# FiLM products by ranges of features, two transposes for the folding products, and a new order of work in a two-layer linear-attention kernel

## The chip, the cores and the metric

The kernel runs on one NeuronCore of one Trainium2 chip. The metric is device time in microseconds of one execution, lower is better. A change is judged against the median of the executions of the kernel before.

## What is computed

Two layers of the same form run one after the other on `x` of shape (32, 128, 512): 32 sequences of 128 positions with 512 features. Layer 0 has 16 heads of 32 features, layer 1 has 8 heads of 64. The masks differ a little; the rest is the same. Cut to what matters:

```python
xn = layernorm(x) * ln_w + ln_b
q, k, v = xn @ Wq + bq, xn @ Wk + bk, xn @ Wv + bv      # k and v masked by position
q = softmax(q per head, over the head's features)
k = softmax(k, over the positions)
att = einsum('bnhd,bnhl->bhdl', k, v)                    # head by head
y = einsum('bnhd,bhdl->bnhl', q, att).reshape(b, t, d)
emb_out = silu(emb) @ W_emb + b_emb                      # FiLM: emb is (32, 1024), W_emb is (1024, 1024)
scale, shift = split(emb_out, 2)
h = layernorm(y) * ln2_w + ln2_b
h = silu(h * (1 + scale) + shift) @ W_out + b_out
x = x + h
```

`emb_out` is the FiLM part. It is computed once for each layer, for all 32 sequences at once: a contraction over 1024 inputs (8 chunks of 128) for 1024 features and 32 rows.

## The kernel before

**Jobs.** The work is cut into 32 jobs: 16 pairs of sequences (`G = 2`) in layer 0, then the same 16 pairs in layer 1. The output of layer 0 goes through DRAM buffers `x1`. All data is float32. Function `job` records one job: normalise the input tile `z`, turn it over into `xnT`, make `k` (tiles `bank_ka`, `bank_kb`, `bank_kc`, `bank_ke`), softmax it, make `q` and `v` (`bank_qa` and so on), multiply `k` by `v` head by head (`bank_pa`), put the results on the diagonal of `att`, multiply by `q` (`bank_py`), normalise `y`, turn it over, apply FiLM and silu into `hT`, make the output (`bank_oa` and so on) and add it to the residual tile `x`.

**Seven products for eight.** In 31 of the 32 jobs each of the three large multiplications is done as seven products of half matrices instead of eight. `sums` forms the sums of halves of the activations (`Sx`, `Sh`, on GpSimd) and `sum_w` those of the weights (VectorE). Products 1, 6 and 7 go into the same PSUM bank `A` one on top of the other, 5 and 3 into bank `E`. Between two products of one bank another engine must have copied or added the bank's content: `kcopy` on ScalarE (line 671), `kadd`, `qcopy`, `qadd` and `oadd` on VectorE. The first job (`plain`) makes the eight products directly (`bank_kp`, `bank_qp`).

**Turning over.** Jobs 1 to 30 (`far`) turn tiles over with VectorE's 32x32 transposes and a round trip through DRAM (`moved`: one write, four reads on the SyncE queue). The first and the last job use TensorE transposes (`bank_xtp`, `bank_tq`, `bank_tk`, `bank_htp`); so does the input of job 1.

**FiLM.** `film` runs once for each layer. For each half `h` of the features and each half of the contraction it loads a 1 MB weight tile `we` and issues four products of 512 columns into `bank_em`, one in each of TensorE's four column groups (lines 479 to 490). Column group `j` holds contraction chunk `j` of the half, so each bank holds four partial sums for 512 features, in 32 partitions each. ScalarE copies the two banks (512 columns each) to the tile `y_e`. Then eight products with a folding matrix `fold` (four 32x32 identities, one above the other; made at the start by `make_fold`, line 373) add up the four partial sums and turn the result over at once, into `bank_etp` (line 498). Five VectorE instructions make the factors `fa` and `fc` of the layer from it.

**Order.** Nothing is issued as it is recorded. `Plan.op` takes each operation with its engine, an assumed duration (`mm`, `dve`, `act`, `pool`) and a due time: the job's base, `31 us` for each job, plus a number at the call, plus a shift from the table `SHIFT`. A row of the table belongs to one call of `op`, its entries to the instances in a job, and its columns to stages of the run: five of them (set-up, job 0, the rest of layer 0, layer 1, the last job). `schedule` then plays the engines in assumed time and picks on each engine, among the operations that can start first, the one due earliest. An operation on another engine's result can start a margin later than the result's assumed end; the margin `SAFE` depends on the engine that makes it (PE 1.35, VectorE 0.01, ScalarE 0.59, GpSimd 0.14, SyncE's transfers 5.62 us). The result is one fixed order of instructions in each engine's queue, and each queue runs strictly in that order.

Of the kernel before, what the change touches and what calls it, by code (L numbers as in the profile page):

```python
# [9 lines left out]
F32 = mybir.dt.float32  # L10
# [6 lines left out]
P = 128  # L17
# [21 lines left out]
    0: ([5.7, 15.9, 47.2, 55.2, 54.4, 44, 62.4, 10.5, 44.1, 62.3], [], [-97.3, -25.3, -45.3, 5.4, 3.3], [53.1, 30.1], []),  # L39
    1: ([], [0.2], [], [], []),  # L40
    2: ([], [27.5], [], [], []),
    3: ([], [-71], [], [], []),
    4: ([], [-16.5], [], [], []),
    5: ([-25.2, 10.4, 32.2, -41.2, 37.7, 6.8, 5.8, 67.3, 87.9, 16.6, -57.5, 31.4], [], [], [-45.1, -59.7, 21.8, -35.8, 14.5, -29, 63.3, 90.6, 5.3, -1.1, -112.2, 10.5], []),
    6: ([], [59.5, 36.8, 59, -24.3, -23.8, -28, 30.3, -17.4, 15.3, -49.7, 36, 7.5], [], [51, 7.4, -32, 18, -64.7, 11.6, 34.3, 28.1, 12.6, 49.7, 53, -39.4], []),
    7: ([-19.6, -17.7], [-47], [-9.4, 28.6], [-38.6, -54.5], [-19.8, -24.4]),
    8: ([-11.2], [], [], [], []),
    9: ([45.5], [], [], [], []),
    10: ([-0.6], [], [], [], []),
    11: ([-22.4], [], [], [], []),  # L50
    12: ([-51.4], [], [], [], []),
    13: ([-16.2, -62.4, 26.5, -36.5], [], [-40.9, -12.9, -23.3, -40.4], [], []),
    14: ([-108.7, -90], [], [2.1, -83.4], [], []),
    15: ([-8.7], [], [4.6], [], []),
    16: ([104.7], [], [41.1], [], []),
    17: ([-29.4], [], [12.6], [], []),
    18: ([-33.1], [], [-51.6], [], []),
    19: ([20.1], [], [57.8], [], []),
    20: ([-16.7], [], [36.6], [], []),
    21: ([98.9], [], [], [], []),  # L60
    22: ([], [-244.7, -141.5, -194.2, -240], [-97.7, -109.1, -130.8, -137, -128.4, -206.2, -333.8, -173.1], [-234, -348.8, -167.7, -71.2, -96.9, -232.6, -243.8, -66.1], [-155.9, -151.5, -127.9, -39.1, -50.7, -147.4, -192, 41.1]),
    23: ([], [], [-39.5, -46.3, -86.4, -246.7], [39, 14.5, 54.9, -63.1], []),
    24: ([], [], [-442.5, -175.6, -223.2, -214.2, -19.7, -47, -249.3, -177.4, -120.6, -199.8, -136, 23.1, -68, -42.8, -24.2, -36.8], [-275.7, -16, -45, 5.7, 48.7, -52.7, -15.7, 46.8, -28.9, -88.2, -92.5, 37.2, 72.2, 63.1, 131.9, 135.8], []),
    25: ([], [96.7, 54.3, 89.8, 65.9], [88.1, 56.4, 71.5, -129.6], [64.2, -41.9, 37.3, -69.5], [152.4, 66.9, 140, 66.9]),
    26: ([], [66.8, 227.4, 94.7, 169.7], [3.6, 121.5, -20.7, 168.3], [92.2, 115.2, 108.5, 168.7], [80.2, 202.2, 126.3, 200.5]),
    27: ([], [-6.3, 19, 65.2, 46.1], [-64.1, -98.9], [-75.4, -19.4], [94.2, 6.6, 70.6, 26.7]),
    28: ([], [-11.3, 64.1, 55.6, 58.2], [-62.3, -13.5], [-12, 223.4], [17.8, 102.7, 102.6, 77.2]),
    29: ([], [], [-38.4, -89.4, -183.3, -77.8], [23.2, -63.7, -92.9, 63], []),
    30: ([], [-91.4, -115.5, -85.1, -68.9], [], [], [-38.6, 6.3, -36.5, -24.9]),
    31: ([], [], [-19.6, 86.2, -70.8, -37.7], [-54.5, 128.2, -100.3, 28.5], []),  # L70
    32: ([], [32], [10.7], [], []),
    33: ([], [], [], [-12.2], [-23.9]),
    34: ([], [-56.2, -118.9], [-3.2, -130.3], [45.7, -29.6], [101.9, 27.4]),
    35: ([], [], [-31.3, -75.6], [133.6, 25.2], []),
    36: ([], [], [-13.5, 0.1, -36.6, 4], [-128.7, -99.9, -92.6, -75.9], []),
    37: ([], [-38, -89.5], [-24.8, -163], [], [10.1, -34.1]),
    38: ([], [16.5, 4, 1.9, -110], [11.8, -31, -3.3, -139.7], [], [-38.3, 29.3, 15.9, -81.1]),
    39: ([], [], [-98.8, -44.3, -29.9, -52.2, -126.4, -36.4, -55.1], [-94, -63.4, -46.1, -24.4, -46, -74.5, -116.1], [-18.2, -14.4, 6.4, 25.4, -11, -12.8, -89.6]),
    40: ([], [], [-135.6, 157.4, 1.7, -182.5, -172.5, 27.1, -156.9, -41.7], [-76.8, -104.5, -102.7, -356.7, -171, -108.9, -44.5, -149.9], [-118.2, -29.9, -61.7, -151.9, -160.7, -51.6, -81.6, -45.2]),
    41: ([], [], [-126.4, -120.8, -91.1, -70.4], [-16.2, -213.7, -208.6, -161.7], [102.4, 6, -7.7, 98.9]),  # L80
    42: ([], [-41.7, -48.3, -58.3, -3.8], [], [], []),
    43: ([], [-36.2, -44.2, 40.1, 28.7], [], [], []),
    44: ([], [19.5, 13.6], [-29.7, 2.1], [-65.6, 73.5], [45.4, 152.5]),
    45: ([], [92.5, -64.9], [-36.9, 13.7], [120.4, 62.2], [56, 143.4]),
    46: ([], [278.9, 169.5, 298.1, 241.9, 215.5, 187.7, 142.9, 298.2], [115, 86.1, 224.4, 228.8, 87, 168, 13.2, 217.3], [132.2, 170.4, 25, 189.7, 235.5, -17.3, 201.8, 243.1], [143.2, 156.6, 168.9, 220.9, 115.8, 118.2, 205, 231.9]),
    47: ([], [-51.7, -40.4], [-41.9, 50], [-168.9, -50.7], [24.8, 27.8]),
    48: ([], [1.5, -27.8], [-51.1, 43.9], [], []),
    49: ([], [], [-33.9, -20.6, -58.3, -10.5, -51.5, -14, -90.1], [-12.2, -35.7, -129.9, -10.7, -150.4, 14.7, -112.4], [107.2, 50.5, 90.7, 151.4, -5.8, 121.5, 87]),
    50: ([], [], [-115.7, -262, -215.8, -197.2], [-66.2, -119.4, -113, -255.5], [58.9, -39.6, 37.1, -113.1]),
    51: ([], [], [-79.6, -42.4, -38.3, -194.8], [-267.2, -385.2, -56.5, -311.8], [-113.2, -76.9, 39.7, -82]),  # L90
    52: ([], [-6.5, 5.2, 9.7, 0.7], [], [], []),
    53: ([], [-28.8, 70.1, -73.2, -24.9], [], [], []),
    54: ([], [53.8, 14.6], [107.1, 142.1], [62.6, -55.6], [140.3, 39.5]),
    55: ([], [-12.9, -44.2], [-30.4, -7.4], [-134.5, -105.7], [-5.9, -86.7]),
    56: ([], [24.2, 12.7], [148, 18], [110.2, 14.9], [150.8, 29.7]),
    57: ([], [-100, -59.5], [-40.2, -215.5], [-57.4, -206.5], [-147.7, 1.5]),
    58: ([], [40.6, -61.7], [58.7, -16.6], [37.6, 22.2], [22.5, 7.6]),
    59: ([], [], [183.4, 30.9], [31.8, 14.3], []),
    60: ([], [], [-63.4, -83.3], [-101.2, -40.5], []),
    61: ([], [54, 121.7], [], [], [88.4, 149.7]),  # L100
    62: ([], [-56.9, -89.1], [], [], [17.4, -47.9]),
    63: ([], [], [24.3, 101.9], [-74.4, -69.5], []),
    64: ([], [85.7, 89.8], [], [], [139.6, 132.8]),
    65: ([], [-95.5, 6.2], [], [], [-37.4, -11]),
    66: ([], [], [], [115.8, -5.1], [16.1, 16.5]),
    67: ([], [24.2], [-66.9], [-103.1], [64.6]),
    68: ([], [91.6, 110.8, 183.2, 28.2], [-19, 34.9, 122.6, 85.8], [], []),
    69: ([], [], [], [-216.7, -240], [-56, -56.5]),
    70: ([], [36.1, 28.6], [-35.5, 19.3], [1.9, -13.1], [61.1, 83.2]),
    71: ([], [-97.2, -39.7], [-173.2, -59.1], [79.7, -119.9], [81.5, 35.6]),  # L110
    72: ([], [], [58.4, 74.4], [118.1, -5], []),
    73: ([], [-75.6, -118.7], [], [], [-36.9, 28.2]),
    74: ([], [-54.5, -51, -83.3, -145, -53.1, -97.2, -81.4, -72.6], [], [], [20.4, 27.6, 36.9, 20.3, 36.4, 12.3, 19.1, -17.8]),
    75: ([], [], [-215.3, -73.1, -108.6, -101.3, -218.9, -167.7, 16.8, 73.8], [-79, -52.3, -191.4, -5.4, -172.2, -78.4, -21.9, 11.5], []),
    76: ([], [18, 16.6, -37.2, -72.2, 56, -24.7, -24.1], [-153.1, -119.4, -159.2, -107.5, -78.7, -115.4, -58.7], [34.2, -35.5, 48.4, 58.4, 57.7, 56.7, -41.8], [126.5, 33.1, 102.9, 80.4, 130.3, 111.6, 94.8]),
    77: ([], [], [], [43, -26.8, -32.4, -4], [18.5, 41, 19.2, 99.5]),
    78: ([], [19.2, 65.2, 30.1, -77.5, -50.7, -22.4, -160, -35.8], [-16.1, 29.3, -4.5, -119.2, -5, -41.5, -138, 18.5], [183.1, 215.1, 162.9, -57.4], [178.7, 285.7, 140.9, 0.5]),
    79: ([], [-62.8], [-25], [15.9], [28.4]),
}


class Buf:


    def __init__(self, kind, name):
        self.kind, self.name = kind, name
        self.ap = None
        self.left = 0
        self.free_at = 0.0
# [23 lines left out]
class Plan:  # L153

    HOP = {"PE": 0.17, "DVE": 0.07, "ACT": 0.07, "POOL": 0.07, "SP": 0.07}

    SAFE = {"PE": 1.35, "DVE": 0.01, "ACT": 0.59, "POOL": 0.14, "SP": 5.62}  # L160
    TAIL = {"PE": 0.13, "DVE": 0.08, "ACT": 0.12, "POOL": 0.08, "SP": 0.0}

    STEP = 31.0

    def __init__(self, nc):
        self.nc = nc
# [136 lines left out]
def dve(n):  # L303
    return 0.074 + n / 970
# [710 lines left out]
```

## Time and profile before

| what | value |
|---|---|
| three executions | 918.66, 919.46, 919.67 us; median 919.46 us |
| the profiled execution | 919.49 us, of which 917.7 us from the first to the last instruction |
| TensorE (PE) | busy 898.7 us, 98% of the span, 6294 matmul records |
| VectorE (DVE) | 767.5 us, 84% |
| ScalarE (ACT) | 633.6 us, 69% |
| GpSimd (POOL) | 535.1 us, 58% |
| DMA | 199.07 MB, mean 217 GB/s |
| FiLM products, `bank_em` | 64 records of 128x512, 32 a layer, in four groups of eight |
| folding products, `bank_etp` | 32 records of 128x32, 16 a layer |

One float32 product is two records in the trace, a TensorE transpose is one. A record's duration is the time from its start to its result; records of one stream overlap, so what a stretch of products costs is read from the start of its first record to the start of what follows. A row of the timeline is: start, duration (us), engine, line, operation, output<-inputs, shapes, number of records, and in brackets the idle time of the engine before it and what ended it.

### The profile page before, as it was taken

Reading aid. Unit: us, or ns where it says so; the run is one execution under the profiler, and the core shown is the slowest. Engines: PE = TensorE matmul, PEld = TensorE weight load, DVE = VectorE, ACT = ScalarE, POOL = GpSimd, SP = SyncE. Lnnn points to the kernel's source line nnn. Section 1 sums busy time; section 2 is a strip of 40 time slices with the busy share of each in tenths; the row PEclk is TensorE's granted clock in tenths of the full one; section 3 lists DMA queues with packets and bytes.
Section 4 is the critical chain, followed back from the end, with each engine's and each line's share of the span. In section 5 each row is a group of like instructions: output and inputs, shape, how many; then the busy total and the mean of one; then the engine's idle time right before and its main releaser. Section 6 shows DMA issues by size and latency. Waiting matters only on the chain.

```text
span 917.7 us, 18442 instructions
## 1 busy us (share of the span) xinstructions
PE 898.7 (98%) x6294; PEld 638.7 (70%) x6294; DVE 767.5 (84%) x1623; ACT 633.6 (69%) x1567; POOL 535.1 (58%) x741
## 2 busy tenths in 40 slices
PE   5999999999999999999999999999999999999996
PEld 4557776767777767776866677677767768676765
DVE  3888879878888888888998989889989879968775
ACT  4467768678687678786677577859778674586581
POOL 3665666656665666665656455457556544554554
PEclk9999999999999999999999999999999999999999
DMA  9747678897977576789776776868688592917542
GB/s 322 241 140 246 179 226 249 240 257 230 276 229 230 179 219 203 236 238 279 234 230 206 256 217 194 253 223 252 215 250 249 170 273 83 266 67 232 176 131 83
DMA packets 126701, 199.07 MB, mean 217 GB/s; under 512 B 13328, under 2 KB 78352, under 8 KB 126608
## 3 DMA queue, kind: packets, MB, share of 16 engines
q1 hardware_dynamic: 126608, 197.90, 69.8%
q8 instruction: 50, 0.82, 0.4%
q14 instruction: 43, 0.35, 0.1%
HBM read 118.68 MB, written 79.17 MB: 216 GB/s over the span
## 4 chain that ended last, share of the span: by engine, by line
PE 98%; DVE 1%; DMA 1%; issue 0%; POOL 0%; SPq 0%; ACT 0%; ACTq 0%
PE bank_qa L739 17%; PE bank_qe L739 12%; PE bank_ka L665 9%; PE bank_oa L913 9%; PE bank_py L868 6%; PE bank_ke L665 6%; PE bank_oe L913 6%; PE bank_qb L739 6%; PE bank_qc L739 6%; PE bank_kc L665 3%; PE bank_oc L913 3%; PE bank_kb L665 3%; PE bank_ob L913 3%; PE bank_pa L847 3%; PE bank_qp L754 1%; PE bank_kp L685 1%
## 5 line engine op out<-in xcount | busy, mean ns | idle before, releaser
L710 POOL TENSOR_TENSOR kT<-kT,mb 128x512 f32<-128x512 f32 x64 | 81.9, 1280 | 93.5 <-DVE kT L676 83.7
L717 ACT ACTIVATE kT<-kT,kmax 128x128 f32<-128x128 f32 x256 | 99.7, 391 | 47.8 <-DVE kmax L713 47.0
L671 ACT ACTIVATE kT<-bank_ka,cols_c 128x128 f32<-128x128 f32 x248 | 76.8, 362 | 74.1 <-PE bank_ka L665 67.5
L739 PE MATMUL bank_qe<-wqv,Sx 128*128 128x512 f32 x248 | 117.2, 595 | 0.0
L739 PE MATMUL bank_qa<-wqv,Sx 128*128 128x512 f32 x248 | 117.0, 594 | 0.0
L780 POOL TENSOR_TENSOR q<-q,qmax 128x512 f32<-128x512 f32 x64 | 66.9, 1046 | 67.6 <-DVE qmax L779 63.4
L899 ACT ACTIVATE hT<-yb,fc_c,fa_c 128x128 f32<-128x128 f32 x240 | 98.8, 482 | 0.4
L553 POOL TENSOR_TENSOR Sx<-xnT 128x256 f32<-128x256 f32 x62 | 44.3, 730 | 57.5 <-PE bank_qe L739 38.7
L553 POOL TENSOR_TENSOR Sh<-hT 128x256 f32<-128x256 f32 x64 | 47.4, 745 | 49.7 <-ACT hT L899 46.9
L739 PEld LDWEIGHTS bank_qa<-wqv,Sx 128*128 128x128 f32 x248 | 45.1, 190 | 42.3 <-issue 38.5
L739 PEld LDWEIGHTS bank_qe<-wqv,Sx 128*128 128x128 f32 x248 | 45.2, 190 | 41.9 <-issue 37.5
L665 PEld LDWEIGHTS bank_ke<-Sx,wk 128*128 128x128 f32 x496 | 63.0, 192 | 14.5 <-issue 11.7
L665 PEld LDWEIGHTS bank_ka<-Sx,wk 128*128 128x128 f32 x496 | 63.3, 192 | 10.5 <-issue 8.4
L868 PEld LDWEIGHTS bank_py<-att_c,qT 128*128 128x128 f32 x512 | 63.6, 192 | 9.6 <-issue 6.7
L633 ACT ACTIVATE xnT<-zb,cols_c 128x256 f32<-128x256 f32 x116 | 61.4, 593 | 10.2 <-PE bank_qc L739 8.8
L868 PE MATMUL bank_py<-att_c,qT 128*128 128x128 f32 x512 | 66.6, 276 | 1.5 <-DVE att_c L856 1.5
L913 PE MATMUL bank_oe<-wo,Sh 128*128 128x256 f32 x256 | 65.9, 380 | 1.7 <-DVE x L923 1.7
L913 PE MATMUL bank_oa<-wo,Sh 128*128 128x256 f32 x256 | 66.0, 381 | 0.8 <-DVE x L919 0.7
L665 PE MATMUL bank_ka<-Sx,wk 128*128 128x128 f32 x496 | 65.9, 276 | 0.0
L665 PE MATMUL bank_ke<-Sx,wk 128*128 128x128 f32 x496 | 65.8, 276 | 0.0
L595 ACT ACTIVATE y<-y,nmrb,rstdb 128x512 f32<-128x512 f32 x60 | 46.7, 805 | 25.9 <-POOL nmrb L583 25.8
L782 ACT ACTIVATE q<-q 128x512 f32<-128x512 f32 x64 | 40.1, 627 | 28.7 <-POOL q L780 28.4
(131 smaller groups left out, 2272.7 us busy)
## 6 DMA issues: line engine op xcount, KB each, us to landing
x<-x SPq DMA_DIRECT2D x32, 512.0 KB, 4.3
qd<-qb SPq DMA_DIRECT2D x30, 512.0 KB, 4.0
kd<-k SPq DMA_DIRECT2D x30, 512.0 KB, 4.2
qb<-qd SPq DMA_DIRECT2D x120, 128.0 KB, 3.4
k<-kd SPq DMA_DIRECT2D x120, 128.0 KB, 3.4
yd<-yb SPq DMA_DIRECT2D x30, 512.0 KB, 3.7
yb<-yd SPq DMA_DIRECT2D x120, 128.0 KB, 3.8
zd<-zb SPq DMA_DIRECT2D x29, 512.0 KB, 3.9
```

Of the source, the lines that this page charges most:

```text
L553: op(22, "POOL", pool(2 * T), lambda i=i, x=x, y=y, f=f: nc.gpsimd.tensor_tensor(S.ap[:, i], x(), y(), f), r, [(S, i)], due=due, lock=True)
L595: op(31, "ACT", act(512, 2, False), lambda: nc.scalar.activation(dst.ap[:, b, :], src.ap[:, b, :], AF.Identity, bias=nmr.ap[:, b : b + 1], ...
L633: op(36, "ACT", act(GT, 2, False), lambda c=c: nc.scalar.activation(xnT.ap[:, c, :].rearrange("p (b r t) -> p r b t", b=G, r=4), zb.ap[:, ...
L665: nc.tensor.matmul(t.ap[:, m * T : (m + 1) * T], kw[quarter].ap[:, c, m * P : (m + 1) * P], a()[:, c, :], start=(first and m == 0 and c == ...
L671: op(40, "ACT", act(T, 1), lambda m=m: nc.scalar.activation(kT.ap[:, 2 * h + m, i, :], Ak.ap[:, m * T : (m + 1) * T], AF.Identity, bias=co ...
L710: op(44, "POOL", pool(2 * GT), lambda hs_=hs_: nc.gpsimd.tensor_tensor(kT.ap[:, hs_].rearrange("p m b t -> p m (b t)"), kT.ap[:, hs_].rear ...
L717: op(46, "ACT", act(T, 1, False) + 0.093, lambda m=m, b=b: nc.scalar.activation(kT.ap[:, m, b, :], kT.ap[:, m, b, :], AF.Exp, bias=km.ap[: ...
L739: nc.tensor.matmul(t.ap, a()[:, c, :], wqv[quarter].ap[:, c, :], start=(first and c == 0), stop=(c == 1), skip_group_check=not first)
L780: op(55, "POOL", pool(512, False), lambda qh=qh, qm=qm: nc.gpsimd.tensor_tensor(qh(), qh(), qm.ap[:, :H].unsqueeze(2).to_broadcast([P, H, ...
L868: nc.tensor.matmul(py.ap[:, m * P : (m + 1) * P], qTc(b, m), att.ap[:, b, m, :], start=True, stop=True)
L899: op(75, "ACT", act(T, 2, False), lambda c=c, b=b: nc.scalar.activation(hT.ap[:, c, b * T : (b + 1) * T].rearrange("p (r t) -> p r t", r=4 ...
L913: nc.tensor.matmul(t.ap[:, :hf], a()[:, c, :], ow[quarter].ap[:, c, :], start=(first and c == 0), stop=(c == 1), skip_group_check=not first)
```

## The change

Three parts. First, in `film` each column group now takes a range of 128 features and the whole contraction: 16 products of 128 columns where there were four of 512. A bank then holds finished sums, 128 columns wide. Second, the copies to `y_e` are 128 columns wide, and two TensorE transposes take the place of the eight products with `fold`; `fold` and `make_fold` are gone. Third, the order is made anew: the `SHIFT` table has new values and eight stages instead of five, and the margins `SAFE` are changed. The calls of `op` after the removed one are numbered one lower.

```diff
 SHIFT = {
-    0: ([5.7, 15.9, 47.2, ...], [], [-97.3, ...], [53.1, 30.1], []),
...
+    0: ([9.3, 8.8, 89.5, ...], [], [], [-101.5], [-101.5, ...], [87.6, 38.9], [87.6], []),
...
-    SAFE = {"PE": 1.35, "DVE": 0.01, "ACT": 0.59, "POOL": 0.14, "SP": 5.62}
+    SAFE = {"PE": 1.21, "DVE": 0.00, "ACT": 0.37, "POOL": 0.31, "SP": 4.87}
...
-        stage = 0 if job < 0 else 1 if job == 0 else 2 if job < B // G else 3 if job < 2 * B // G - 1 else 4
+        stage = 0 if job < 0 else 1 + (job > 0) + (job > 1) + (job > 3) + (job >= B // G) + (job >= 2 * B // G - 2) + (job == 2 * B // G - 1)
...
-    fold = fixed("fold", [P, B])
...
-    def make_fold():
-        for j in range(P // B):
-            nc.vector.tensor_copy(fold.ap[j * B : (j + 1) * B, :], ident.ap[j * B : (j + 1) * B, j * B : (j + 1) * B])
-    op(3, "DVE", 0.5, make_fold, [ident], [fold])
...
                 def go(h=h, half=half, w=w):
                     for j in range(4):
-                        nc.tensor.matmul(
-                            e[h].ap[j * B : (j + 1) * B, :],
-                            cT.ap[:, 4 * half + j, :],
-                            w.ap[:, j, :],
-                            start=(half == 0),
-                            stop=(half == 1),
-                            tile_position=(0, j * B),
-                        )
+                        for g in range(4):
+                            nc.tensor.matmul(
+                                e[h].ap[g * B : (g + 1) * B, :P],
+                                cT.ap[:, 4 * half + j, :],
+                                w.ap[:, j, g * P : (g + 1) * P],
+                                start=(half == 0 and j == 0),
+                                stop=(half == 1 and j == 3),
+                                tile_position=(0, g * B),
+                            )
...
-            op(14, "ACT", act(512), lambda h=h: nc.scalar.copy(esb.ap[:, h, :], e[h].ap), [e[h]], [(esb, h)], due=14)
+            op(13, "ACT", act(P), lambda h=h: nc.scalar.copy(esb.ap[:, h, :P], e[h].ap[:, :P]), [e[h]], [(esb, h)], due=14)
...
         def total():
-            for c in range(NE):
-                nc.tensor.matmul(
-                    tp.ap[:, c * B : (c + 1) * B], esb.ap[:, c // NC, c % NC * P : (c % NC + 1) * P], fold.ap, start=True, stop=True
-                )
-        op(15, "PE", mm(NE, B), total, [esb, fold], [tp], due=15)
+            for h in range(2):
+                nc.tensor.transpose(tp.ap[:, h * P : (h + 1) * P], esb.ap[:, h, :P], ident.ap)
+        op(14, "PE", mm(2, P, True), total, [esb, ident], [tp], due=15)
```

## The prediction

> **What bounds the kernel now.** I read the page first, for the engine whose time the end hangs on:
>
> ```profile
> PE 898.7 (98%) x6294; PEld 638.7 (70%) x6294; DVE 767.5 (84%) x1623; ACT 633.6 (69%) x1567; POOL 535.1 (58%) x741
> ...
> PE 98%; DVE 1%; DMA 1%; issue 0%; POOL 0%; SPq 0%; ACT 0%; ACTq 0%
> ```
>
> The chain that ended last is TensorE for 98% of the span. The busy time by stages (columns: stretch, its length, PE, PEld, DVE, ACT, POOL, granted clock, DMA share, GB/s) and TensorE's waits tell where the rest is:
>
> ```profile
> 0.00:14.34 14.34, 4.04 (x16) 3.10 (x16) 6.29 (x16) 4.67 (x8) 5.12 (x17) 1.00 0.86 288
> 14.34:36.00 21.66, 21.66 (x98) 15.46 (x98) 12.47 (x22) 11.69 (x32) 11.93 (x14) 1.00 0.94 328
> 36.00:885.00 849.00, 848.97 (x6006) 601.30 (x6005) 731.53 (x1548) 604.30 (x1494) 504.09 (x694) 1.00 0.71 218
> 885.00:917.70 32.70, 24.01 (x178) 18.82 (x176) 17.20 (x39) 12.99 (x37) 13.95 (x18) 0.98 0.27 91
> ```
>
> ```profile
> PE bank_xtp L644 <- DVE z L591: 9.1, 1, 9.1
> PE bank_oe L913 <- DVE x L923: 1.7, 2, 1.1
> PE bank_py L868 <- DVE att_c L856: 1.5, 1, 1.5
> PE bank_xtp L644 <- ACT z L595: 1.1, 1, 1.1
> PE bank_oa L913 <- DVE x L919: 0.7, 1, 0.7
> ```
>
> From 14.3 to 885 us TensorE is never idle; all its waits are in the first 13 and the last 30 us. So a microsecond taken out of TensorE's stream anywhere ends the kernel a microsecond earlier, a new order can win only at the two ends, and in the middle it can only lose.
>
> **The change, part by part.** The sum is made against the profiled execution, 919.49 us, which is 0.03 above the median of the three, 919.46. These rows of the timeline price the FiLM part (two rows for each stretch: its first record, and what comes after it):
>
> ```profile
> 29.67 1.06 PE L482 MATMUL bank_em<-we,cT_c 128*32 128x512 f32 x8
> 30.67 1.16 PE L665 MATMUL bank_kc<-xnT,wk 128*128 128x128 f32 x8
> ...
> 84.94 1.87 PE L498 MATMUL bank_etp<-fold_c,y_e 128*128 128x32 f32 x16
> 86.64 1.14 PE L868 MATMUL bank_py<-att_c,qT 128*128 128x128 f32 x8
> ...
> 847.26 1.10 PE L847 MATMUL bank_pa<-v,k 128*32 128x64 f32 x64
> 848.29 0.66 PE L644 MATMUL bank_xtp<-ident_c,z 128*128 128x128 f32 x4
> ...
> 888.68 0.60 PE L824 MATMUL bank_tk<-ident_c,kT 128*128 128x128 f32 x4
> 889.12 0.60 PE L805 MATMUL bank_tq<-ident_c,q 128*128 128x128 f32 x4
> ```
>
> *Folding products out, transposes in.* The folding products take TensorE from 84.94 to 86.64, 1.70 us, and the same again at 238.78: 3.40 us. Four transposes of 128x128 take from 888.68 to 889.12, 0.44 us; the change adds two a layer, 0.22, so 0.44 in all. Gain 2.96 us.
>
> *FiLM products.* Eight records of 512 columns in four column groups take 1.00 us (29.67 to 30.67): two rounds, 1024 columns for each group. The new form is 32 records of 128 columns: eight rounds, again 1024 columns for each group. The packed products of layer 1 are the same form of instruction (128x32 weights, column groups in turn) with 64 columns: 64 records, sixteen rounds, 1024 columns for each group, 1.03 us. Eight rounds lie between two and sixteen, so between 1.00 and 1.03: I take 1.02. There are eight such groups: +0.15 us (0 to +0.24).
>
> The `bank_pa` row says that the weight loads between small products hide: sixteen rounds of 64 columns cost only 0.03 us more than two of 512, with 64 loads instead of 8. [...]
>
> *Copies and folding matrix.* The four copies of `bank_em` (567 to 600 ns each) become four times narrower, and `make_fold` leaves VectorE. ScalarE is idle for 31% of the span, and VectorE waits for `z` after `make_fold`: nothing on the path.
>
> *Order, start.* ScalarE's queue of the changed kernel normalises the first half of job 1's `z`, then makes two of job 0's `xnT`, then normalises the second half. In the kernel before, both halves come first:
>
> ```profile
> 10.96 1.52 ACT L595 ACTIVATE z<-z,nmra,rstda 128x512 f32<-128x512 f32 x2 [1.59 <-POOL nmra L583]
> 12.38 3.73 ACT L648 ACTIVATE xnT<-bank_xtp,cols_c 128x256 f32<-128x256 f32 x8
> ...
> 12.53 1.97 PE L644 MATMUL bank_xtp<-ident_c,z 128*128 128x128 f32 x8 [1.08 <-ACT z L595]
> 14.34 5.83 PE L685 MATMUL bank_kp<-xnT,wk 128*128 128x256 f32 x16
> ```
>
> The transposes of job 1 wait for both halves, and behind them on TensorE stand all products. Two `xnT` are 2 x 0.47 = 0.94 us, so the first product starts at 15.28, not 14.34. It now needs two tiles of `wqv` that are issued right after the mask; in the trace of before 2.6 MB had landed by 10.6 us, about what has to come first now, so that is no wait. One thing can change the 0.94: TensorE is slow at first, which its records show and the granted clock here (1.00) does not. The first sixteen `kp` records take 5.67 us (14.34 to 20.01), the eight at 23.52 take 1.73; the pace doubles at 18.7. If that moment stays, the delay costs half, +0.47; if it moves along, +0.94; I take +0.9, as the activity starts later. [...]
>
> *Order, end.* In the kernel before the last three gaps of any size are 0.60 us before `bank_oe` of job 13, 1.51 before `bank_py` of job 15 (two VectorE instructions make `att`), and 1.79 at the last two products. The changed order puts that `bank_oe` (0.86 us) between `bank_pa` and `bank_py`: it covers 0.86 of the 1.51 and loses its own 0.60, a gain of 1.46. Against it, the last product for job 15's `v` now has only one output product and one transpose group (0.86 + 0.44) between it and `bank_pa`, where it had 5.7 us. What lies between is an addition of 0.69 and a masking of 0.72, which in the trace of before end 1.9 us after that product (886.96 to 888.85): a wait of 0.6. Two smaller ones come where VectorE, which must first turn over `y` of job 14, reads the banks of that `v` and of job 13 late: about 0.5 together. After `bank_py` both orders have the same chain of output products and additions. Net -0.4 (-1.5 to +1.0).
>
> *Order, middle.* 0 before; after, between 0 and what the rival below gives. The planner's margin is smaller by 0.14 us for TensorE's results, 0.22 for ScalarE's and 0.75 for transfers. The page's `L671` group shows ScalarE idle 74 us in front of the bank copies, 67.5 of it ended by TensorE: copies mostly start at once. I take +0.1.
>
> Sum: 919.49 - 2.96 + 0.15 + 0.9 - 0.4 + 0.1 = 917.28, say **917.3 us**.
>
> **Rivals.**
> *Slower: bank copies held up on ScalarE.* Product 6 of `k` adds to the bank that product 1 filled, so two copies of 0.36 us must be over; with the hand-overs that is about 1.1 us. In layer 0 the TensorE work between the two falls from a median of 18 us to 7, and its smallest from 4.4 to 2.6. In jobs 10, 13 and 16 (3.3 to 3.5 us) the copies stand behind exponentials of the job before, which wait for GpSimd's masking (1.28) and VectorE's maximum (0.68). Once those come more than 3.4 - 1.1 = 2.3 us late, TensorE stands, with everything behind it. Three such jobs at 2 us each are +6: 923.3. For it: ScalarE already waits 47.0 us for `kmax` in front of its exponentials (group `L717`). Against it: the trace of before has jobs at 3.5 and 3.8 without a wait.
>
> *Faster: the ends recovered.* If the new order also fills the last gaps (1.79) and the start costs half: 917.28 - 1.79 - 0.43 = 915.1. Against it: the last additions form one chain in both orders.
>
> *No change that shows.* FiLM gives 2.8, but start and middle take 1.5 to 4 of it: 918 to 920. A measurement of this kernel can tell about 0.2%, 1.8 us, from no change. [...]
>
> **How the numbers follow.** The forecast (915.9 to 918.3) has 0.50, the faster rival 0.15, no change that shows 0.17, the slower rival (921.5 up) 0.18. Faster by over 0.2% means under 919.46 - 1.84 = 917.6: that is 0.7 of the forecast's own range, 0.35, and with the faster rival 0.50. The rest of the forecast (0.15) and most of the third case give 0.30 for the same; the slower rival and a little of the third 0.20. The range of 8 in 10 goes from 914.3 (the faster rival with a better tail) to 922.5 (the slower one with two or three jobs held up).
>
> **What would show it.** Right: `bank_etp` as 4 records in 0.44 us over both layers; `bank_em` groups of 32 records in 1.00 to 1.03 us; first product at 15.3; no TensorE wait between 36 and 885 us. Wrong: groups of 1.2 us or more (loads don't hide), a row `bank_ka <- ACT kT` in TensorE's waits (the slower rival), or a first product at 14.3.

## The result and the profile after

The changed kernel takes 915.76 us (median of 6 runs, 915.36 to 916.24). The kernel before, run beside it, takes 918.94 (6 runs, 917.81 to 919.67): a ratio of 0.9967, 95% interval 0.9954 to 0.9979, so 3.2 us less (1.9 to 4.2). The forecast was 917.3 with a range of 914.3 to 922.5. The profiled execution took 915.75 us with a span of 913.9, 3.74 less than the 919.49 of before.

The page of the changed kernel, with the engines' busy time and the shares of the chain that ended last:

```profile
PE 895.5 (98%) x6458; PEld 640.1 (70%) x6458; DVE 770.1 (84%) x1619; ACT 629.9 (69%) x1565; POOL 536.1 (59%) x741
...
PE 97%; DVE 1%; ACT 1%; DMA 1%; POOL 1%; issue 0%; SPq 0%; ACTq 0%
```

TensorE has 164 records more and is busy 3.2 us less; it still carries the end. The stages (cut at the new first product, 15.00 us) and TensorE's waits:

```profile
0.00:15.00 15.00, 3.99 (x16) 3.30 (x17) 4.65 (x12) 5.18 (x8) 5.44 (x17) 1.00 0.86 291
15.00:36.00 21.00, 21.00 (x117) 14.74 (x117) 12.56 (x21) 11.31 (x31) 12.94 (x12) 1.00 0.77 278
36.00:885.00 849.00, 848.69 (x6168) 605.76 (x6167) 736.99 (x1552) 603.83 (x1506) 504.30 (x696) 1.00 0.70 220
885.00:913.90 28.90, 21.77 (x160) 16.32 (x158) 15.94 (x37) 9.59 (x21) 13.46 (x17) 0.89 0.23 86
```

```profile
PE bank_xtp L636 <- DVE z L583: 8.8, 1, 8.8
PE bank_xtp L636 <- ACT z L587: 2.1, 1, 2.1
PE bank_oe L905 <- DVE x L915: 1.1, 1, 1.1
PE bank_oa L905 <- DVE x L911: 0.7, 1, 0.7
PE bank_py L860 <- DVE att_c L848: 0.5, 1, 0.5
PE bank_qe L731 <- DVE wqv L399: 0.3, 1, 0.3
PE bank_pa L839 <- ACT v L823: 0.2, 1, 0.2
```

At the start the wait for ScalarE's `z` grew from 1.1 to 2.1. In the middle there is one new wait, 0.3 us (at 51.0 us), and no `bank_ka`. At the end the wait before `bank_py` fell from 1.5 to 0.5, one of the two before `bank_oe` (0.6) is gone, and a small one before `bank_pa` (0.2) is new. In the last stretch the granted clock is 0.89, where it was 0.98. The rows of the timeline behind this (three of before first, then those of the changed kernel):

```profile
891.62 1.13 PE L913 MATMUL bank_oe<-wo,Sh 128*128 128x256 f32 x4 [0.60 <-DVE x L923]
...
895.29 2.05 PE L868 MATMUL bank_py<-att_c,qT 128*128 128x128 f32 x16 [1.51 <-DVE att_c L856]
...
911.94 1.10 PE L913 MATMUL bank_oe<-wo,Sh 128*128 128x256 f32 x4 [1.12 <-DVE x L923]
```

```profile
10.77 0.81 ACT L587 ACTIVATE z<-z,nmra,rstda 128x512 f32<-128x512 f32 x1 [1.75 <-POOL nmra L575]
11.49 1.00 ACT L640 ACTIVATE xnT<-bank_xtp,cols_c 128x256 f32<-128x256 f32 x2
12.38 0.81 ACT L587 ACTIVATE z<-z,nmra,rstda 128x512 f32<-128x512 f32 x1
...
15.00 4.55 PE L746 MATMUL bank_qp<-wqv,xnT 128*128 128x512 f32 x8
...
33.40 1.08 PE L476 MATMUL bank_em<-we,cT_c 128*32 128x128 f32 x32
34.41 1.98 PE L731 MATMUL bank_qa<-wqv,xnT 128*128 128x512 f32 x4
...
82.70 0.38 PE L492 MATMUL bank_etp<-ident_c,y_e 128*128 128x128 f32 x2
82.92 1.06 PE L657 MATMUL bank_ka<-xnT,wk 128*128 128x128 f32 x8
...
888.02 1.10 PE L839 MATMUL bank_pa<-v,k 128*32 128x64 f32 x64 [0.23 <-ACT v L823]
889.05 1.13 PE L905 MATMUL bank_oe<-wo,Sh 128*128 128x256 f32 x4
890.63 2.05 PE L860 MATMUL bank_py<-att_c,qT 128*128 128x128 f32 x16 [0.46 <-DVE att_c L848]
...
905.34 1.10 PE L905 MATMUL bank_oa<-wo,Sh 128*128 128x256 f32 x4 [0.66 <-DVE x L911]
907.56 1.82 PE L905 MATMUL bank_oe<-wo,Sh 128*128 128x256 f32 x4 [1.12 <-DVE x L915]
```

Two `xnT` stand between the two halves of `z`. A group of 32 `em` records takes 1.01 us (33.40 to 34.41), and the two transposes of a layer 0.22 (82.70 to 82.92; the same at 256.51). The last `bank_oe` takes 1.82 us, where the same four records took 1.10 before: TensorE ran most of it at half pace, since the granted clock is 0.50 from 907.80 on.

**One number before the comparisons.** In these traces TensorE runs at half pace until the first entry of the granted clock, its release: eight transposes of the start hold it for 1.76 us before the release (13.24 to 15.00 in the changed kernel) and for 0.87 after it (13.72 to 14.59 in `warm_filled`, below). With R for the moment of the release, a stream of products that starts at F and is released at R ends like one that started at full pace at E = (F + R)/2 (E = F if R is earlier). R is 18.66 before, 16.92 after. So E is (14.34 + 18.66)/2 = 16.50 before and (15.00 + 16.92)/2 = 15.96 after, and the span less E is what the stream itself takes: 901.17 and 897.98. Two executions can differ in E by luck, as the experiments show; in the span less E the traces differ far less.

### The profile page after: what moved, and what is told of

Same layout as the page of the kernel before. It is cut to its first block, busy times and chain, and to the rows that moved or that the text cites. A ratio compares the mean times of both kernels' runs of the same rounds, so it can differ in the third digit from the quotient of the medians.

```text
span 913.9 us, 18761 instructions
## 1 busy us (share of the span) xinstructions
PE 895.5 (98%) x6458; PEld 640.1 (70%) x6458; DVE 770.1 (84%) x1619; ACT 629.9 (69%) x1565; POOL 536.1 (59%) x741
## 4 chain that ended last, share of the span: by engine, by line
PE 97%; DVE 1%; ACT 1%; DMA 1%; POOL 1%; issue 0%; SPq 0%; ACTq 0%
PE bank_qa L731 18%; PE bank_qe L731 12%; PE bank_ka L657 9%; PE bank_oa L905 9%; PE bank_ke L657 6%; PE bank_py L860 6%; PE bank_oe L905 6%; PE bank_qc L731 6%; PE bank_qb L731 6%; PE bank_kc L657 3%; PE bank_kb L657 3%; PE bank_oc L905 3%; PE bank_ob L905 3%; PE bank_pa L839 3%; PE bank_qp L746 2%; PE bank_em L476 1%
## 5 line engine op out<-in xcount | busy, mean ns | idle before, releaser
L731 PE MATMUL bank_qa<-wqv,xnT 128*128 128x512 f32 x124 | 58.7, 596 | 0.0
```

The lines of the kernel that those rows point to most:

```text
L731: nc.tensor.matmul(t.ap, a()[:, c, :], wqv[quarter].ap[:, c, :], start=(first and c == 0), stop=(c == 1), skip_group_check=not first)
```

## The experiments

**The two parts, each alone.** The first kernel keeps the order of before (every engine's list) and has the new FiLM products, copies and transposes; the second has the changed order with the old FiLM:

```diff
-                        nc.tensor.matmul(
-                            e[h].ap[j * B : (j + 1) * B, :],
...
+                        for g in range(4):
+                            nc.tensor.matmul(
+                                e[h].ap[g * B : (g + 1) * B, :P],
...
-            for c in range(NE):
...
+            for h in range(2):
+                nc.tensor.transpose(tp.ap[:, h * P : (h + 1) * P], esb.ap[:, h, :P], ident.ap)
```

That is the diff of film_old_order against before; the same lines the other way round, and `make_fold` put back, are that of old_film_new_order against after.

> The FiLM change alone, in the order of the kernel before (each engine's list of instructions is that of before, with 32 em products where there were 8, narrower copies, and two transposes in place of eight folding products). Theory 1 (the two parts add up): the traces give -2.96 for the folding products and +0.12 for the em groups, so 2.85 us less than before, about 916.1. Theory 2 (the old order was made for the old lengths, and the time saved turns into waits): 1 to 2 us less, 917 to 918, with new TensorE waits between 36 and 885 us. Theory 3 (most of the change's gain is the new order's): under 1 us less.

Measured: 915.60 (5 runs), ratio 0.9964 (0.9951 to 0.9976): 3.3 us less (2.2 to 4.5).

> The new order alone: the changed kernel's order with the old em products (512 columns), the old copies and the folding products. Theory 1 (the parts add up): the changed kernel plus 2.85 us, about 918.6, so 0.3 to 0.9 us less than before. Theory 2 (the new order holds only with the short FiLM): above 919.5. Theory 3 (the order brings most of the gain): 916 to 917.

Measured: 918.97 (11 runs), ratio 0.9996 (0.9987 to 1.0005): no difference. So the FiLM change brings the gain, and the new order is worth about nothing as a whole; theory 1 of both kernels stands on the sum, but the intervals are as wide as the order's share. The traces are finer: span less E is 914.70 - 16.09 = 898.61 for the first and 917.65 - 17.46 = 900.19 for the second, against 901.17. The FiLM change takes 2.56 out of the old order's stream, the new order alone 0.98. In the profiled execution of the second kernel E is 17.46, 0.96 later than in that of before (16.50), which takes the 0.98 back; the medians, 918.97 against 919.08, say that this is so in general.

**The clock at the start.** Idle transposes of the identity, which nobody reads, go into TensorE's waits of the start. WARM is {0: 26, 1: 30} in the changed kernel and {0: 26, 1: 20} in the kernel before:

```diff
                 def go(c2=c2, tp=tp):
+                    for _ in range(0 if L else WARM.pop(j, 0)):
+                        nc.tensor.transpose(tp.ap[:, :P], ident.ap, ident.ap)
```

> The changed kernel, with transposes of the identity that nobody reads in TensorE's two waits of the start: 26 ahead of the first xtp group, 30 ahead of the second; everything else as it was. Theory 1 (the clock is released after a stretch in which TensorE works without a break, so work in the waits brings it forward): full pace before the first product; the eight second transposes take 0.85 less, and 0.96 of slow products goes: first product at about 14.15 instead of 15.00 us, 1.8 us less than the changed kernel, about 914.0. Theory 2 (the release comes at a moment that the program doesn't move): first product still at 15.0, no change, 915.8. Theory 3 (released, but lost again): between the two.

Measured: 914.18 (5 runs, 913.32 to 915.74), ratio to before 0.9951 (0.9937 to 0.9965). The clock is released at 7.58 us, the first product starts at 14.59, at full pace (0.44 later than theory 1 had it), and the span less E is 911.88 - 14.59 = 897.29. That is theory 1 in the profiled execution, 913.74 us. Two of the five, 915.40 and 915.74, are no faster than the unfilled kernel; they left no trace, and theory 3 (released and lost again) is open for them.

> The kernel before with the same filling (26 and 20 transposes). Theory 1 (the start's share of the change is the moment of the clock's release and nothing else): first product at 13.5 instead of 14.34 us and none of them slow (2.2 us lost in the profiled execution), so 2.5 to 3.0 us less than before, about 916.2; the filled changed kernel is then 2.2 to 2.6 us faster than this one, less than the 3.2 between the unfilled ones, because the later first product (0.7) is left without its cover. Theory 2 (the new start order is faster by itself): the two filled kernels differ by 3.2 us or more.

Measured: 918.50 (11 runs, 916.93 to 919.32), ratio 0.9993 (0.9985 to 1.0002), 2.3 us above the 916.2 expected. The stretches of its trace, cut at multiples of 3.413 us from the release (from the release to the loss of the clock it is 897.71 us in before and 890.88 in the changed kernel, 263 and 261 times as long), show why (columns as in the stages: length, PE, PEld, DVE, ACT, POOL, granted clock, DMA share, GB/s):

```profile
4.07:7.48 3.41, 3.33 (x16) 2.92 (x14) 1.70 (x5) 0.00 (x0) 0.79 (x3) 1.00 1.09 330
7.48:10.90 3.42, 1.54 (x12) 1.35 (x13) 2.45 (x7) 1.28 (x1) 2.19 (x6) 1.00 0.96 316
10.90:14.31 3.41, 3.41 (x18) 3.41 (x17) 0.69 (x1) 3.33 (x6) 0.27 (x2) 0.50 1.07 420
14.31:17.72 3.41, 3.41 (x22) 3.13 (x21) 0.00 (x0) 2.47 (x6) 0.70 (x1) 1.00 1.09 366
```

The clock is released at 7.48, after a full step (3.33 of 3.41). The next is less than half busy (1.54), and the clock is at 0.50 in the one after it, in which the idle transposes themselves are slow (twenty of them, from 10.51 on, take 4.01 us, and 2.35 in `held_both_ends`) and push the first product to 15.24. Release, loss and second release (7.48, 10.90, 14.31) lie on one grid of 3.413 us. Span less E is 916.38 - 15.24 = 901.14, that of before to 0.03. So what sets the starts of these two executions of the old order apart lies in E, and the stream behind it is the same.

**The start held.** Filling for any position of the grid, in both orders (in the old order WARM is {0: 46, 1: 12}, and the identity comes first there anyway):

```diff
-    1: ([], [-49.4], [], [], [], [], [], []),
+    1: ([], [-120], [], [], [], [], [], []),
...
+WARM = {0: 46, 1: 20}
```

> The changed kernel with the identity made first and with 46 and 20 idle transposes in TensorE's two waits of the start, so many that whatever the phase of the 3.413 us steps is, the first group ends after the release and the second is over before the second half of z arrives. Theory 1 (the moment of release falls on a grid of 3.413 us that lies differently in each execution; a step of unbroken work releases the clock, a step with half of it idle takes it back): first product at 14.1 to 14.2 us at full pace in every execution. Unfilled, the stream starts at 15.0 and is released between 16.65 and 20.05, which costs the same as a start at full pace at 15.8 to 17.5, 16.65 on the mean; so 2.4 us less than the changed kernel, about 913.3, and its times lie within 1 us of each other, where those of before cover 2.15 us. Theory 2 (the spread has another cause, transfers for example): the spread stays at 2 us.

Measured: 914.63 (914.18 to 915.01), ratio 0.9950 (0.9937 to 0.9962). The spread is 0.8 us as theory 1 has it, but this decides nothing: the six executions of the unfilled changed kernel cover 0.9 as well. What speaks for theory 1 is the clock in the traces (put together below). The time is 1.3 above its 913.3. In the profiled execution `z` arrived late (the first group started at 9.29, after 8.76) and put the first product at 14.72, and a step with half of it idle ended at 906.8, so that the last four records ran at half pace (1.80 us). Span less E is 912.88 - 14.72 = 898.16, and without the 0.70 that these lost, 897.46.

> The FiLM change under the old order, with the clock held at the start in the same way (46 and 12 idle transposes): the two orders compared without the clock's phase. First product at about 14.35 us, 0.2 later than in the changed order so filled. Theory 1 (the new order's end is 1.5 us shorter, its middle 0.3 longer): 914.3 to 914.8, so 1.2 to 1.5 us more than the filled changed kernel. Theory 2 (the two orders are worth the same, as new order alone against before, 918.97 to 919.08, might say): within 0.4 us of it.

Measured: 915.26 (914.47 to 916.24), ratio 0.9954 (0.9940 to 0.9967): 0.6 more than `held`. Between the theories: its profiled execution had a half-idle step too, which ended at 907.3 (last four records 1.70 us, 0.60 too long). Span less E is 914.46 - 14.11 = 900.35, 1.74 more than in `film_old_order` with the same stream. 0.60 of it is that product; the other 1.15 lie behind the last product, from whose end to the end of the span it is 5.78 us, against 4.56 to 4.63 in `before`, `after` and `film_old_order`. What took them is open. The end had to be held as well.

**Both ends held.** 5 and 9 idle transposes more ahead of the last two products, into a bank that is read out already:

```diff
             def go():
+                if (j, L) == (B // G - 1, 1):
+                    for _ in range({7: 5, 3: 9}.get(i, 0)):
+                        nc.tensor.transpose(tp.ap[:, :P], ident.ap, ident.ap)
```

> The filled changed kernel, with 5 and 9 idle transposes more in the two waits ahead of the last two products. Theory 1 (in the profiled execution of the changed kernel a step with half of it idle ended at 907.8, and the last four records ran at half pace, 0.72 us; this meets about one execution in four): 0.1 to 0.2 us less on the mean than with the start filled alone, never over 0.3 above the fastest; last bank_oe product in 1.10 us, not 1.82. Theory 2 (the idle transposes delay the products behind them): 0.2 us more or worse.

```profile
902.44 0.71 PE L909 MATMUL bank_htp<-ident_c 128*128 128x128 f32 x5
903.27 1.10 PE L911 MATMUL bank_oa<-wo,Sh 128*128 128x256 f32 x4
904.21 1.15 PE L909 MATMUL bank_htp<-ident_c 128*128 128x128 f32 x9
905.49 1.10 PE L911 MATMUL bank_oe<-wo,Sh 128*128 128x256 f32 x4
```

Measured: 913.60 (912.98 to 914.07), ratio 0.9938 (0.9926 to 0.9950): 1.0 us under `held`, more than expected, and its times cover 1.1 us, not 0.3. The last product takes 1.10, and the waits ahead of both are covered. Of the 1.73 us between the two profiled spans (912.88 and 911.16) this is worth 0.7; the other 0.99 lies in the earlier first product (13.73 against 14.72), as `z` came earlier, which the filling of the end can't have caused. So the 1.0 is no clean price of the filling. This is the fastest version: 5.7 us under the kernel before, and about 2.7 under the changed kernel if the two ratios (0.9938 and 0.9967) are set against each other; the two did not run side by side. Span less E: 911.16 - 13.73 = 897.43.

The same holding with the old FiLM, and with the old order (there with 9 transposes ahead of `bank_py` too):

> The new order with the old FiLM (512-column products, folding products), and the clock held at both ends as in the kernel held_both_ends (913.6 us, 912.98 to 914.07): the FiLM change by itself, with the clock's phase out of the comparison. Theory 1 (the traces: -2.96 for the folding products, +0.12 for the em groups): 2.85 us more than held_both_ends, 916.3 to 916.6. Theory 2 (the 3.5 us between before and the FiLM change under the old order are real): 3.3 us more or over, 916.9 up.

Measured: 916.63 (11 runs, 915.94 to 918.01), ratio 0.9980 (0.9971 to 0.9989): 3.0 above `held_both_ends` by the medians, and 900.20 - 897.43 = 2.77 by span less E. The two did not run side by side, and by their ratios to before (0.9980 and 0.9938) the difference is 3.9, so the times alone decide for neither theory. The traces say theory 1.

> The FiLM change under the old order, with the clock held at the start (46 and 12 idle transposes) and at the end (9 ahead of bank_py of job 15, 5 and 9 ahead of the last two products): the order by itself, with the clock's phase out of the comparison. The waits of 0.60 and 1.51 us for data stay. Theory 1 (the new order's end is 1.47 shorter, its middle 0.3 longer, the starts alike once the clock is released early): 1.0 to 1.3 us more than held_both_ends, 914.6 to 914.9. Theory 2 (the order is worth nothing): within 0.3 of 913.6.

Measured: 914.64 (914.37 to 915.26), ratio 0.9956 (0.9944 to 0.9969): 1.0 above by the medians, 1.7 by the ratios (again not side by side), and 898.62 - 897.43 = 1.19 by span less E. Theory 2 fits none of the three; by the traces it is theory 1, and the new order's stream is 1.2 shorter.

The traces in one table (span less E, us; `held` and `held_old_order`, with their slow last products, are given above):

| | old order | new order |
|---|---|---|
| old FiLM | 901.17 (before), 901.14 (warm_filled_before) | 900.19 (old_film_new_order), 900.20 (held_old_film) |
| new FiLM | 898.61 (film_old_order), 898.62 (held_old_order_ends) | 897.29 (warm_filled), 897.43 (held_both_ends), 897.98 (after, with its slow last product) |

**The moved product of the end, undone.** `bank_oe` of job 13 goes behind `bank_py` of job 15; the order on the other engines stays:

```diff
+        late = [o for o in todo if o.key == (29, 75, 6)]
+        at = max(i for i, o in enumerate(todo) if o.key[:2] == (31, 69))
...
+        todo = [o for o in todo[: at + 1] if o not in late] + late + rest
```

> The changed kernel with one group of four products (bank_oe of job 13) moved behind bank_py of job 15, so that nothing stands between bank_pa and bank_py; all other instructions in their places. Theory 1 (this product covers 0.86 of the wait for att): TensorE stands 1.3 to 1.5 us before bank_py instead of 0.46, and the last product starts 0.9 us later after bank_pa than before. Theory 2 (att comes earlier when VectorE is not busy with the bank of bank_oe): the wait grows by less than 0.5.

One execution: 919.32 us, span 917.5. The rows of its timeline, its waits and the two steps around `bank_py`:

```profile
887.69 1.10 PE L849 MATMUL bank_pa<-v,k 128*32 128x64 f32 x64 [0.23 <-ACT v L833]
890.30 3.60 PE L870 MATMUL bank_py<-att_c,qT 128*128 128x128 f32 x16 [1.51 <-DVE att_c L858]
893.70 1.15 PE L915 MATMUL bank_oe<-wo,Sh 128*128 128x256 f32 x4
...
898.80 1.10 PE L915 MATMUL bank_oa<-wo,Sh 128*128 128x256 f32 x4 [1.35 <-DVE x L921]
```

```profile
PE bank_oa L915 <- DVE x L921: 2.0, 2, 1.4
PE bank_py L870 <- DVE att_c L858: 1.5, 1, 1.5
```

```profile
887.11:890.53 3.42, 1.68 (x70) 1.27 (x68) 2.92 (x7) 3.39 (x6) 1.31 (x2) 1.00 0.02 5
890.53:893.94 3.41, 3.41 (x17) 3.41 (x17) 0.00 (x0) 2.08 (x6) 1.90 (x3) 0.50 0.00 0
```

The wait is back at 1.51, as theory 1 has it: `bank_oe` covered 1.05 of it. But the last product starts 23.26 us after `bank_pa` (910.95), where it was 19.54: 3.7 later, not 0.9. That has two causes nobody had priced. The addition of `bank_oe` still stands ahead of `bank_py`'s product on VectorE's queue, so `y` of job 15 now waits for it, and a new wait of 1.35 follows before `bank_oa`; this part belongs to the edit, which left VectorE's order alone. And the wait made its step half idle (1.68 of 3.42), so the clock fell to 0.50 and `bank_py` took 3.60 instead of 2.05. The same wait of 1.51 in the kernel before cost no clock: the step it ended in was 0.56 busy (1.90 of 3.41).

**The loops of the FiLM products exchanged.**

```diff
-                    for j in range(4):
-                        for g in range(4):
+                    for g in range(4):
+                        for j in range(4):
```

> The changed kernel with the two loops of the em products exchanged: the four products of one column group follow each other, and then those of the next group, instead of the four groups in turn. Same products, same sums. Theory 1 (small products run side by side only when neighbours in the queue go to different column groups): a group of 32 records costs up to 32 x 110 ns = 3.5 us instead of 1.01, 20 us more for the kernel. Theory 2 (side by side in whatever order): 1.0 us a group, no change. Theory 3 (side by side, but weight loads no longer hide): between the two, 1.5 to 2 us a group.

```profile
34.59 2.46 PE L476 MATMUL bank_em<-we,cT_c 128*32 128x128 f32 x32
36.98 1.98 PE L731 MATMUL bank_qa<-wqv,xnT 128*128 128x512 f32 x4
```

One execution: 926.65 us. A group takes 2.39 us (34.59 to 36.98) instead of 1.01, for the same 32 records: for eight groups 8 x 1.38 = 11.0 us, and the time is 10.9 over that of the changed kernel. That is between theory 1 and theory 2, and above the 1.5 to 2 of theory 3. The record starts tell it from theory 3: neighbours of one column group start 109 ns apart, and in the changed kernel each round of four starts 109 ns after the one before, so a load costs no more here than there (its median is 110 ns in both). What is lost is most of the side by side: the eight records of a column group start one after the other, and the first of the next column group starts beside the fifth. The four column groups in turn are what makes the new form as cheap as the old (1.01 us a group against 1.00).

## Why the prediction was right, and where it was off

**FiLM: right.** -2.96 + 0.15 was predicted, -2.81. The four transposes take 0.44 us in all against 3.40, and the `em` groups went from 1.00 to 1.01, so -2.85 by the rows; the new order keeps 2.77 (held_old_film). The old order keeps only 2.56: at 238 us a wait for VectorE's `v` behind `bank_py` delays the product behind it by 0.29 (0.13 of it shows as idle time). The row of the packed products, sixteen rounds in 1.03 us, led the prediction to 1.02 a group, and the measured 1.01 confirms it.

**Start: the size was right, its sign in this pair was luck.** The first product was to start 0.94 later, at 15.28, and the start to cost 0.9. It stands 6.16 to 6.27 us behind the first transpose in the four unfilled kernels with the new start (after, old_film_new_order, oe_after_py, em_by_group) and 5.24 and 5.37 in the two with the old one: 0.9. That it started at 15.00 and not 15.28 is an earlier `z` (8.76 after, 9.11 before), which varies from 8.38 to 9.46 between the traces. And E, which is what counts, fell by 0.54, since the release came 3.7 us after the second group started in one execution and 6.1 us in the other.

In the trace of the changed kernel the clock is taken back at 907.80, 890.88 us after its release: 261 steps of 3.413. In that of before it is taken back at 916.36, behind the last product and 897.71 us after its release: 263 steps. Counted in such steps, by the time that products are busy in them, the clock was released after 3.41 of 3.41 us (15.25 to 18.66 in before, 13.51 to 16.92 in the changed kernel), after 3.42 of 3.42 (`warm_filled`) and after 3.33 of 3.41 (`warm_filled_before`), and not after 2.72 of 3.41 (11.84 to 15.25 in before). It was taken back after 1.64 of 3.42 (the changed kernel), 1.68 of 3.42 (`oe_after_py`) and 1.54 of 3.42 (`warm_filled_before`), and kept after 1.90 of 3.41 (892.47 to 895.88 in before) and 2.12 of 3.41 (`warm_filled`). These steps show nothing between. The grid lies differently in each execution: the releases at 18.66 (before), 16.92 (after), 7.58 (`warm_filled`) and 7.48 us (`warm_filled_before`) are 1.59, 3.27, 0.75 and 0.65 past a multiple of the step. So, as an estimate from these traces, R comes about one to two steps after the unbroken stretch begins (3.4 to 6.8 us; 3.7 to 6.1 in the six unfilled traces), and E varies by up to half a step, 1.7 us. That would be most of the 2.7 that 51 executions of before cover (917.61 to 920.33); no run separates it from the rest, for example the arrival of `z`.

On the mean, with R one and a half steps (5.12 us) after the unbroken stretch begins, E is 0.5 x (5.24 + 3.42 + 5.12) = 6.9 us after `z` in the old order and 0.5 x (6.24 + 4.48 + 5.12) = 7.9 in the new: an estimate from these rows of +1.0, where +0.9 was predicted. The runs agree: old_film_new_order has a stream 0.98 shorter than before and a median only 0.11 lower, so its start cost about 0.9.

**End: the term that was mis-sized.** -0.4 was predicted, made of -1.46, +0.6 and +0.5. The first was right: the own wait of 0.60 is gone and 1.51 became 0.46, -1.65. The step that failed is the two against it. The wait for `v` is 0.23, not 0.6: its masking ends 1.64 us after the product (886.32 to 887.96) and not 1.9, as it no longer stands behind an exponential on ScalarE. And VectorE reads the banks of `v` and of job 13 in time, so the 0.5 is not there. By the waits, 0.60 + 1.51 became 0.23 + 0.46: -1.42, at the better end of the range. With the 0.3 of the middle that is -1.1, and the traces give the new order's stream as 0.98 to 1.19 shorter. The slow last product (+0.72) that hides half of this in the profiled execution belongs to the grid and not to the order: `held` in the new and `held_old_order` in the old order had it too.

**Middle: small, as forecast, but not nothing.** +0.1 was predicted, and among the signs of being right stood no wait between 36 and 885 us; one of 0.31 at 51.0 us (`wqv` sums on VectorE) is there. The slower rival's `bank_ka` waits don't exist.

**The sum.** -2.85 + 1.0 - 1.42 + 0.3 = -3.0, and 3.2 less was measured. The forecast's -2.2 lacked the 1.0 of the end, and it was set against an execution of 919.49 that stands 0.6 above the median of the 51 (918.93), with its release late in what the grid allows (6.1 us after the second group started). The time came out between the forecast and the faster rival (915.1), and not for that rival's reason: the last gaps stayed (0.7 and 1.1).

## What to carry to other kernels

Before two executions are compared, take out what the clock's step gave each: with the start of full pace subtracted, traces of the same stream agreed here to 0.14 us where the last product ran at full pace. Look at what follows the last product too: in `held_old_order` it took 1.15 more. Price a wait on the busiest engine at more than its length if it makes a step half idle (here 1.55 us more for a wait of 1.51), and fill it with work that nobody reads, if that work surely ends before the wait does; `warm_filled_before`, whose filling was too short for the grid, gained nothing that its interval shows. When small products, as here, are to run side by side in column groups, let the groups alternate in the innermost loop (here 1.01 us for 32 records, and 2.39 with the loops exchanged).

## What the runs showed of the hardware that was not expected

A wait of 1.51 us in front of `bank_py` cost 1.55 more through the clock in `oe_after_py`, where it left its step 0.49 busy, and nothing in the kernel before, where its step was 0.56 busy. Four products in a row to one column group are not fully one after the other either: 2.39 us for 32 records, where 32 x 0.11 would be 3.5, as the next column group starts beside the second half of the one before.
